# An attention layer's sums begun inside the decay layer before it: grouped decay sums, a norm in two parts, degrees on VectorE

## The chip, the cores and the metric

The kernel runs on one core of one Trainium2 chip. Its time is the device time of one execution in microseconds (us), the median over the runs of one kernel. The engines are called TensorE (matmuls, PE in the profile), ScalarE (ACT), VectorE (DVE), GpSimd (POOL) and SyncE (SP, which issues most of the DMAs). Each works through its own queue and waits on the others by semaphores.

## The reference

A graph network of four layers over N = 3327 nodes with D = 64 features and a 0/1 adjacency matrix of 3327 x 3327, some 0.5% ones. Each layer adds its result to x after `h = relu(layernorm(x))`. Layers 0 and 3 are hyperbolic attention layers; the change leaves their work as it is. Cut to the two middle ones:

```python
# layer 1, decay: a node's last neighbours count, each half as much as the next
support = h @ weight
rank = cumsum(adj != 0, axis=1)
k = minimum(rank[:, -1:], 100)
pos = rank - (rank[:, -1:] - k)
w = (adj != 0) * where(pos > 0, 0.5 ** (k - pos), 0)
x = x + w @ support + bias
# layer 2, attention with two GRU cells (h = relu(layernorm(x)) again)
A = adj - diag(diag(adj))
edge = gru([(A > 0) @ h, (A < 0) @ h], h)
att = softmax(where(A > 0, e_plus, where(A < 0, e_minus, -9e15)))
node = gru((att * A) @ (h @ W), h)
x = x + diag(adj)[:, None] * edge + diag(adj)[:, None] * node
```

Since the adjacency is 0 or 1, the softmax of layer 2 is an average over the neighbours: both cells need only the plain sums `A @ h` and the degrees. The kernel counts whether each entry is 0 or 1 (`ok`, `zo`) and has a general path for other inputs, which doesn't run here.

## The kernel before, in words

The nodes are padded to 26 blocks of 128 (T = 26, NP = 3328). The transposed adjacency is kept on chip as 13 pairs of masks in an 8-bit type (`masks`), which layers 1 to 3 use. Features stand as `X[p, t, d]` (node t * 128 + p), in two halves o = 0, 1 of 13 blocks each.

**Decay, `plain_decay` (L1358).** Work goes in 52 steps: c = 0, 1 is a half of the columns, and inside it the blocks b run from 25 down to 0. Step k needs one adjacency tile of 832 KB (`quarters(k)`, 128 x 2 x 832). Tiles 0 to 11 are made into masks during layer 0; tiles from 12 on are loaded into seven buffers in rotation (`bufs`: four made in layer 0 and three more). `make_mask(k)` turns a tile into its mask, on GpSimd or, for some tiles, on VectorE, three steps ahead; `check(k)` counts its zeros on VectorE and then loads tile k + 7 into the buffer. A list `LATE` names 12 tiles that aren't checked here; they are loaded again in the attention layer and checked there.

A step's TensorE work is counting and summing. `counts(k, o, after)` adds, into a PSUM tile `cnt[o]`, how many neighbours come later than each one; ScalarE's exponential (`weights`, L1425) makes the decay's weights `w` from it; `counts(k, o, rest)` brings the counter forward to the next block, and so must wait until that exponential has read it. `sums(k)` (L1430) multiplies the weights with the features of block b, given as two 16-bit parts, into `acc[c]`. Steps 0 to 11 only count, while the features are being made (L1549 to L1558). From k = 12 the loop at L1540 runs counts of step k and sums of earlier steps: two sums each step ahead of the counts until it has caught up, later one sum between the counts. The weights `w` lie in 13 places: ten inside masks not yet made and three of their own. When a half is done, `degrees` (L1441) reads the degrees from `cnt[o]` on ScalarE, `out_of` copies the sums to `outP`, and `from_pairs` multiplies them with the layer's weights and adds the result to X, in pieces: for the first six blocks of each half inside the loop (k = 29, 32), for the other seven after it.

**Attention, `plain_gat` (L1606).** First the norm of all 26 blocks (`norm_relu`, L136: sums, centred values, squares on ScalarE, a square root with a correction, then h and its two 16-bit parts), then on the first of TensorE's banks the product of two small weight matrices (L1643 to L1649: transpose of `wg`, a ScalarE copy `wgT`, a matmul, a ScalarE copy into `wx`), then the sums: 26 blocks of 16 matmuls (L1708) with b from 25 to 0, and between the blocks, by the table `todo`, transposes of H (`turn`), corrections of the degrees (`degrees`), the late checks and the inverse of the degrees (`inverse`). Then eight steps of the two GRU cells (2 cells x 4 column pieces, L1776 to L1794: `products` on TensorE, `sigmoids`, `tanh` on ScalarE, `before_tanh`, `state` on VectorE), and last `from_pairs`, which turns the result, scales it by the diagonal and adds it to X (L1796 to L1803).

**What sets the order.** Layer 0 opens a region with `tc.manual_schedule` for ScalarE, VectorE, TensorE and GpSimd (L576), in which every engine's queue has the order in which the Python text issues the instructions; `plain_decay` runs in it. `plain_gat` is called after that region has ended and opens its own for ScalarE, VectorE and TensorE (L1632), around the norm, the sums and the GRU steps; its last `from_pairs` stands outside, so that the planner places those instructions. DMAs on SyncE go out in order, each when its buffer is free.

## Time and profile before

| what | value |
| --- | --- |
| median of 3 runs (lowest, highest) | 750.41 us (749.41, 752.73) |
| the profiled execution | 750.64 us |
| its span, first to last instruction | 748.8 us |
| TensorE busy (matmul), VectorE, ScalarE, GpSimd | 634.7, 518.6, 543.1, 467.3 us |
| mean granted TensorE clock | 0.947 |
| layer 0 / decay / attention / layer 3 in the span, about | 0 to 239 / 239 to 393 / 393 to 487 / 487 to 749 us |

"Busy" is the time in which an engine had an instruction under way. The page also gives the chain of work that ended last, followed back from the last instruction; a span on it can be shortened only by shortening what is on it or by starting it earlier. Idle time of an engine off that chain costs nothing. In rows of the timeline, the first number is the start in us and the second the length in us; in the chain too.

### The profile page before, as it was taken

How to read it: one execution, taken by the hardware profiler on the slowest of the kernel's cores; microseconds unless marked ns; L12 is line 12 of the kernel's file. 1: busy time of each engine (PE TensorE's matmuls, PEld its weight loads, DVE VectorE, ACT ScalarE, POOL GpSimd, SP SyncE). 2: the span in 40 equal slices, each digit the busy share in tenths (PEclk: the TensorE clock that was granted, in tenths of full speed). 3: DMA queues.
4: the chain of work that ended last, by engine and by line, in shares of the span. 5: the costliest groups of instructions: out<-in, count | busy, mean ns of one | idle time of the engine just before them, and what ended most of it. 6: DMA issues, size and time to landing. Idle time of an engine off the chain costs nothing.

```text
span 748.8 us, 11837 instructions
## 1 busy us (share of the span) xinstructions
PE 634.7 (85%) x4227; PEld 257.6 (34%) x4227; DVE 518.6 (69%) x909; ACT 543.1 (73%) x697; POOL 467.3 (62%) x353
## 2 busy tenths in 40 slices
PE   0799999999999788889982999328999999999950
PEld 0522233333333333434441663124223333333310
DVE  6867777777777698978828577996555555555556
ACT  2788888888887864577782369257888889889841
POOL 2699989989999002399910000036888788887830
PEclk9999999999999999999995999659999999999995
DMA  3988898988888600599813640001001001000001
GB/s 62 347 261 284 267 279 252 287 273 275 259 261 266 260 1 10 200 401 380 334 36 149 223 143 1 0 0 39 1 1 39 1 2 38 0 1 1 1 2 49
DMA packets 57028, 106.46 MB, mean 142 GB/s; under 512 B 8928, under 2 KB 33152, under 8 KB 56960
## 3 DMA queue, kind: packets, MB, share of 16 engines
q1 hardware_dynamic: 52608, 105.59, 42.5%
q10 hardware_dynamic: 4352, 0.02, 0.3%
q8 instruction: 35, 0.57, 0.3%
q14 instruction: 33, 0.27, 0.1%
HBM read 102.87 MB, written 0.88 MB: 139 GB/s over the span
## 4 chain that ended last, share of the span: by engine, by line
PE 59%; DVE 18%; ACT 8%; issue 7%; POOL 5%; DMA 1%; ACTq 1%; POOLq 0%; DVEq 0%
PE slot L627 16%; PE slot L635 9%; PE slot L608 8%; PE slot L1422 7%; PE slot L609 7%; PE bank L1708 5%; POOL sig L597 5%; PE slot L1436 4%; ACT sig L595 2%; DVE X L1473 2%; DMA adj<-in 1%; DVE mask L1410 1%; ACT slot L614 1%; ACTq L307 1%; ACT w L1428 1%
## 5 line engine op out<-in xcount | busy, mean ns | idle before, releaser
L618 DVE SCALAR_TENSOR_TENSOR sig<-slot,sig 128x768 f32<-128x768 f32 (+1 forms) x208 | 212.7, 1022 | 145.7 <-POOL sig L597 141.7
L614 ACT ACTIVATE slot<-slot 128x768 f32<-128x768 f32 (+1 forms) x208 | 177.3, 852 | 54.4 <-PE slot L609 54.2
L597 POOL TENSOR_TENSOR sig<-adj,sig 128x768 f32<-128x768 f32 (+1 forms) x104 | 201.0, 1962 | 14.2 <-ACT sig L595 10.0
L595 ACT ACTIVATE sig<-leftB,right 128x768 f32<-128x768 f32 (+1 forms) x208 | 203.2, 977 | 0.1
L597 POOL TENSOR_TENSOR sig<-mask,sig 128x768 f32<-128x768 fp8e4 (+1 forms) x104 | 173.2, 1677 | 40.4 <-ACT sig L595 35.0
L627 PE MATMUL slot<-sig,Xr 128*64 128x384 f32 (+1 forms) x832 | 169.6, 526 | 6.3 <-DVE sig L618 6.1
L608 PE MATMUL slot<-XC,XT 128*128 128x384 f16 (+1 forms) x416 | 142.2, 342 | 3.2 <-ACT sum L645 1.7
L609 PE MATMUL slot<-XF,XE 73*128 73x384 f16 (+1 forms) x416 | 141.4, 340 | 0.0
L635 PE MATMUL slot<-sig,X 128*32 128x384 f32 (+1 forms) x832 | 94.2, 525 | 0.0
L1428 ACT ACTIVATE w<-slot,ebias 128x832 bf16<-128x832 f32 x76 | 68.6, 951 | 30.7 <-PE slot L1422 30.6
L627 PEld LDWEIGHTS slot<-sig,Xr 128*64 128x64 f32 x832 | 49.6, 135 | 88.0 <-issue 61.5
L608 PEld LDWEIGHTS <-XT 128*128 128x128 f16 x416 | 40.6, 98 | 93.8 <-issue 67.4
L1422 PE MATMUL slot<-mask,rest 128*128 128x416 fp8e4 x208 | 55.0, 347 | 8.3 <-ACT mask L1428 4.2
L1413 POOL CAST mask<-ahead 128x1664 fp8e4<-128x1664 f32 x17 | 27.8, 1642 | 49.5 <-PE slot L1436 45.1
L1422 PE MATMUL slot<-mask,after 128*128 128x416 fp8e4 x208 | 54.7, 346 | 4.4 <-ACT deg L1443 2.9
L418 POOL MEMSET X<- 128x832 f32 x2 | 1.6, 791 | 84.4 <-ACT xh L1732 84.4
L1333 DVE TENSOR_SCALAR_CACHE_REDUCE same<-ahead 128x832 bf16<-128x832 f32 (+1 forms) x39 | 52.4, 1345 | 0.3
L609 PEld LDWEIGHTS <-XE 73*128 73x128 f16 x416 | 40.8, 98 | 29.7 <-issue 5.6
L1333 DVE TENSOR_SCALAR_CACHE_REDUCE same<-adj 128x1664 bf16<-128x1664 f32 x25 | 47.1, 1882 | 0.6
L1708 PE MATMUL bank<-mask,h 128*64 128x416 fp8e4 x416 | 40.1, 353 | 0.0
L635 PEld LDWEIGHTS slot<-sig,X 128*32 128x32 f32 x832 | 16.4, 108 | 67.7 <-issue 66.1
L1428 ACT ACTIVATE mask<-slot,ebias 128x832 bf16<-128x832 f32 x28 | 26.1, 952 | 11.5 <-PE slot L1422 11.3
(315 smaller groups left out, 636.6 us busy)
## 6 DMA issues: line engine op xcount, KB each, us to landing
adj<-in SPq DMA_DIRECT2D x78, 384.0 KB, 4.5
adj<-in SPq DMA_DIRECT2D x28, 832.0 KB, 6.8
ahead<-in SPq DMA_DIRECT2D x20, 832.0 KB, 8.3
adj<-in SPq DMA_DIRECT2D x27, 512.0 KB, 4.9
ahead<-in SPq DMA_DIRECT2D x32, 416.0 KB, 5.2
leftB<-left SPq DMA_DIRECT2D x6, 384.0 KB, 3.4
XC<-XT SPq DMA_DIRECT2D x12, 96.0 KB, 5.5
X<-in SPq DMA_DIRECT2D x2, 416.0 KB
```

Of the source, the lines that this page charges most:

```text
L595: A.activation(sig, leftB[c], AF.Sigmoid, bias=right[:, b:b + 1])
L597: G.tensor_tensor(sig, adj, sig, op=OP.mult)
L608: PE.matmul(L[:, o, :c[1] * P], XT[:, rows], XC[c][:, o, :], start=True, stop=False)
L609: PE.matmul(L[:, o, :c[1] * P], XE[:KE, rows], XF[c][:, o, :], start=False, stop=True)
L614: A.activation(L, L, AF.Arctan, scale=PA / SX ** 2)
L618: V.scalar_tensor_tensor(sig, slot[:, :, :tiles[k][0][1] * P], PC, sig, op0=OP.add, op1=OP.mult)
L627: PE.matmul(acc[c][o * D:(o + 1) * D, 0, :n], Xr[:, b, :], sigs[k][:, o, :], start=b == 0, stop=b == T - 1)
L635: PE.matmul(acc[c][q:q + 32, 1, :n], X0[:, b - 1 + i, :], w[:, o, :], start=b == 1, stop=b == T - 1, tile_position=(0, q))
L1333: V.tensor_scalar(same, adj, 0.0, 0.0, op0=OP.is_equal, op1=OP.add, accum_out=count)
L1422: PE.matmul(cnt[o][:, h, :BK], w, cols(k, o, h), start=w is after and steps[k][1] == T - 1, stop=True, skip_group_check=True)
L1428: A.activation(ws[k][:, o, :, :], cnt[o][:, :, :BK], AF.Exp, scale=-LN2, bias=ebias)
L1708: PE.matmul(acc[k][o * D:(o + 1) * D, :], w, mask[:, o * HP + k * BK:o * HP + (k + 1) * BK], start=b == T - 1 and i == 0, stop=b == 0 and ...
```

## The change

* **Loop of the decay.** Counts of step k always come first. Sums follow them in groups: in the first half four at every second step (two at the last ones), in the second half four at k = 30, 34, ..., 50 and the last two at k = 52. The weights have five places of their own instead of three.
* **Degrees.** All but the first of the four degree copies move from ScalarE to VectorE.
* **The tiles.** Tiles 39, 43 and 47 leave `LATE`: they are checked in the decay and not loaded again. Two of the seven tile buffers are allocated outside of layer 0's room (`own`); from step 26 on no new tile is loaded into them, and H and its two 16-bit parts are written there.
* **Norm of the first 12 blocks inside the decay.** `normed_h` is a generator whose pieces are issued one per step from k = 33 on, for blocks 0 to 5 of each half; it uses ScalarE's logarithm and exponential for the inverse root. Their table set is loaded at k = 24; the table load for the square root after the loop goes.
* **The attention's sums** take blocks 0, 13, 1, 14, ... in the order in which their norm is ready. `plain_gat` is called from inside the decay's region. Three blocks are issued between the last two `from_pairs` of the decay, then the norm of the other 14 blocks (`finish`), then the small weights' product and blocks 3 to 25 with a new table `todo`. The PSUM banks of the decay are used on. The late tiles are loaded after `finish`.
* **The end of the GRU.** The four pieces of the last `from_pairs` are issued inside the GRU loop after `state(5)`, `state(6)` and `state(7)`, in the ordered region.
* The diagonal products on GpSimd go one per two steps from k = 25 on, instead of one per step.

```diff
-    LATE = *range(EARLY, EARLY + 4), *range(EARLY + 7, 2 * T - 4, 4)
+    BY_V = range(EARLY + 7, 2 * T - 4, 4)
+    LATE = *range(EARLY, EARLY + 4), *BY_V[:5]
...
-            for k in (1, 0, 4, 3, 2):
...
-            own = [pers.tile([P, 2, 2, BK], BF, name=f"w{i}") for i in range(3)]
+            for k, q in ((1, 0), (0, 0), (0, 1), (1, 1), *[(k, q) for k in (4, 3, 2) for q in range(2)]):
+                free.append(masks[k].bitcast(BF)[:, q, :].rearrange("p (o h i) -> p o h i", o=2, h=2))
+            own = [pers.tile([P, 2, 2, BK], BF, name=f"w{i}") for i in range(5)]
...
             def check(k):
                 if k not in LATE:
-                    zeros(same, adj_of(k), zo[:, k:k + 1])
-                load(k + len(bufs))
+                    zeros(same, adjs[k], zo[:, k:k + 1])
+                buf = adjs.pop(k)
+                if k < T or not any(buf is t for t in ah_.own):
+                    load(next(coming), buf)
...
-                A.activation(deg[q, c * CW:(c + 1) * CW].rearrange("p (h i) -> p h i", h=2),
-                             cnt[o][q, :, :BK], AF.Copy, accum_out=zo[q, 2 * T + c:2 * T + c + 1])
+                if c == 0 and o == 0:
+                    A.activation(to, cnt[o][q, :, :BK], AF.Copy, accum_out=total)
+                else:
+                    V.tensor_scalar(to, cnt[o][q, :, :BK], 1.0, 0.0, op0=OP.mult, op1=OP.add, accum_out=total)
...
+            def normed_h(ks, mid, squares):
...
+                V.reduce_sum(s, x, axis=AX.X)
+                yield
+                V.tensor_scalar(s, s, 1.0 / D, None, op0=OP.mult)
+                yield
+                V.tensor_sub(mid, x, wide4(s))
+                yield
+                A.activation(squares, mid, AF.Square)
+                yield
+                V.reduce_sum(v, squares, axis=AX.X)
+                yield
+                V.tensor_scalar(v, v, 1.0 / D, LN_EPS, op0=OP.mult, op1=OP.add)
+                yield
+                A.activation(y, v, AF.Ln)
+                A.activation(y, y, AF.Exp, scale=-0.5)
+                yield
+                V.scalar_tensor_tensor(q, y, -0.5, y, op0=OP.mult, op1=OP.mult)
+                yield
+                V.tensor_mul(q, q, v)
+                yield
+                V.scalar_tensor_tensor(y, q, 1.5, y, op0=OP.add, op1=OP.mult)
+                yield
+                for o in range(2):
+                    V.scalar_tensor_tensor(to[:, o], mid[:, o], 0.0, y[:, o, :, None].to_broadcast([P, n, D]),
+                                           op0=OP.max, op1=OP.mult)
+                    A.activation(hi[:, o], to[:, o], AF.Copy, scale=SH)
+                    yield
+                for o in range(2):
+                    V.scalar_tensor_tensor(lo[:, o], to[:, o], SH, hi[:, o], op0=OP.mult, op1=OP.subtract)
+                    yield
...
-            for k in range(LAG, K_ + 2):
+            norm0 = normed_h(slice(0, T // 4), M[:, :12, :], Xr[:, :12, :])
+            for k in range(LAG, K_ + 1):
                 c, b = steps[min(k, K_ - 1)]
-                if done < k - 1:
-                    for _ in range(2):
-                        sums(done)
-                        done += 1
-                    catching = True
-                else:
-                    catching = False
                 if k < K_:
                     counts_before(k)
-                elif k == K_:
+                else:
                     counts(k - 1, 1, rest)
                     degrees(steps[k - 1][0], 1)
+                if k in (T - 4, T) or k < T and k % 2 == 0 or k > T and (k - T) % 4 == 0 or k == K_:
+                    n = k if k in (T - 4, T, K_) else min(done + 4, k)
+                    for i in range(done, n):
+                        sums(i)
+                    done = n
+                    if done in (T, K_):
+                        out_of(0 if done == T else 1)
...
-                if not catching and done < K_:
-                    sums(done)
-                    done += 1
-                    if steps[done - 1][1] == 0:
-                        out_of(steps[done - 1][0])
...
+                if k == T - 2:
+                    A.preload_act_table_set("natural_log_exp_and_others")
+                if k > T + 6:
+                    next(norm0, None)
+            for _ in norm0:
+                pass
+            drop_diagonal(masks[0][:, 0, :], 0, 0, NP)
+
+            def last_x(i):
                 pt = acc[0][:, i, :].rearrange("p (t h d) -> p t h d", h=2, d=D)
-                from_pairs(None, outP, add, wt, ts, pt)
...
+                from_pairs(None, outP, add, wt, (range(6, 10), range(10, T // 2))[i], pt)
+
+            def finish():
+                for _ in normed_h(slice(T // 4, T // 2), M[:, :14, :], Xr[:, 12:, :]):
+                    pass
...
+            order = [o * C2 + k for ks in (range(T // 4), range(T // 4, C2)) for k in ks for o in range(2)]
...
+            block(0)
+            last_x(0)
+            block(1)
+            last_x(1)
+            block(2)
+            finish()
+            close()
             wk = st.enter_context(room(name="pgl", bufs=4))
...
-                todo = {T - 2: lambda: check(3), T - 4: lambda: turn(0), T - 6: lambda: degrees(0, 1),
-                        T - 7: lambda: check(2), T - 8: lambda: turn(4), T - 10: lambda: degrees(2, 3),
-                        T - 11: inverse, T - 12: lambda: turn(8), T - 15: lambda: turn(12)}
...
+                todo = {4: lambda: turn(0), 5: lambda: check(1), 6: lambda: degrees(0, 1), 8: lambda: check(3),
+                        9: lambda: degrees(2, 3), 11: inverse, 13: lambda: turn(4), 15: lambda: turn(8),
+                        17: lambda: turn(12)}
+                for n in range(3, T):
+                    block(n)
+                    if n in todo:
+                        todo[n]()
...
+                def last(i):
+                    from_pairs(None, oP, use, None, range(4 * i, min(4 * i + 4, C2)),
+                               banks[4 + i].rearrange("p (t h d) -> p t h d", h=2, d=D))
...
-                from_pairs(ps, oP, use)
+                    for i in {C + 2: (0,), C + 3: (1,), C + 4: (2, 3)}.get(u, ()):
+                        last(i)
```

In the diff `V`, `A`, `G` and `PE` are VectorE, ScalarE, GpSimd and TensorE. The small weights' product (`wgT`, `wx`) is unchanged and now stands after `close()` and before block 3.

## The prediction

> **What bounds the kernel now.** I read the page first (span, then the chain by line), then the chain in order of time between 236 and 516 us, where every edited line runs, then the waits there, and last the separate queues of TensorE, ScalarE and VectorE. The two outer layers (0 to 238 and 512 to 749 us) keep their instructions, so only these 275 us are costed. From the chain (start, length, what):
>
> ```profile
> 380.37 1.51 PE slot L1422 x8
> 381.89 0.82 PE slot L1436 x8
> 382.71 1.51 PE slot L1422 x8
> ...
> 387.88 0.95 ACT deg L1443 x2
> ...
> 394.65 1.96 DVE ln_s L144 x2
> ...
> 407.75 0.04 issue
> 407.80 0.90 PE bank L1648 x2
> 408.70 8.02 PE bank L1708 x64
> ...
> 435.27 15.09 PE bank L1708 x170
> 450.38 0.51 ACT xh L1726
> ```
>
> The decay's second half is TensorE work without a hole: 8 counting matmuls and 8 summing ones, 1.51 + 0.82 = 2.33 us a step. Then TensorE leaves the chain for some 19 us (degrees, last outputs, the norm), and the attention's sums run from 408.70 to 450.38. Removing that hole is what there is to win. The waits there say what TensorE resumes on, and the queues show the rhythms that the change runs into (ScalarE, TensorE, VectorE; start, length, operation):
>
> ```profile
> PEld bank L1648 <- ACT wgT L1645: 13.8, 1, 13.8
> ```
>
> ```profile
> 256.16 11.43 ACT L1428 ACTIVATE mask<-slot,ebias 128x832 bf16<-128x832 f32 x12
> ```
>
> ```profile
> 300.79 1.60 PE L1436 MATMUL slot<-mask,h 128*64 128x416 bf16 x16
> 302.32 0.53 PE L1422 MATMUL slot<-mask,after 128*128 128x416 fp8e4 x2
> ```
>
> ```profile
> 324.77 1.89 DVE L1333 TENSOR_SCALAR_CACHE_REDUCE same<-ahead 128x1664 bf16<-128x1664 f32 x1
> ...
> 478.46 0.58 DVE L1773 TENSOR_TENSOR o<-o,gate 128x416 f32<-128x416 f32 x1
> 478.96 0.68 DVE L1801 TENSOR_TENSOR o<-pt,dcol 128x512 f32<-128x512 f32 x1
> 479.56 0.58 DVE L1774 TENSOR_TENSOR H<-o,nn 128x416 f32<-128x416 f32 x1
> ```
>
> TensorE waited for the copy of wgT, which stands in ScalarE's queue behind the norm's copies. In steps without sums (k = 4 to 11) ScalarE sets the pace: 12 exponentials in 11.43 us, so 1.905 us a step. Sixteen summing matmuls take 302.32 - 300.79 = 1.53 us, eight take 0.83: each further eight cost 0.70 and a change of kind 0.13. The last fence is VectorE in step 26 (a check of an adjacency tile) and at the end of the GRU, where the output's L1801 is woven between two operations of one state.
>
> **What the Trainium skill says.** "PSUM — Partial Sum Buffer", Engine vs sequencer instructions: ScalarE's and VectorE's queues are strictly first in, first out, and matmuls start in program order. The 13.8 us agree. "TensorE: Matmul & The Clock Gate", What's actually happening: an idle window of about 3.4 us halves TensorE's clock. Here the granted clock is 0.50 through 408.5 to 413 us, and 64 matmuls take 8.02 us where 64 x 0.088 = 5.6 are due: 2.4 us lost. "ScalarE: Activation LUTs", Table sets: one set holds both ln and exp; the trace's loads are 1.28 us each.
>
> **The change, part by part.** S(k) is the start of step k's first counting pair; before, S27 = 327.92, S30 = 335.60, S34 = 345.62, S50 = 383.06, S51 = 385.40.
>
> *First half, grouped sums.* Up to 298.7 VectorE's norm and masks hold TensorE, unchanged. From there pairs of steps cost 4.42 + 1.91 = 6.3 us with four sums, against 2 x 3.60; but the masks of steps 24 and 25 are ready only at 316.7 and 319.9 (their casts on GpSimd, behind DMA). Sum: 0, S26 near 323.4 (323.57 before). The table load at k = 24 (1.28 us) falls under the sums there, when ScalarE has about 1.4 us free. Without them, +1.3.
>
> *Degrees.* The trace has no 64x832 VectorE copy out of PSUM; L1447's 384 and 512 elements (0.55, 0.69) give about 1.05 plus 0.08 for the accumulator, near ScalarE's 0.86 + 0.20: between -0.1 and +0.3. What matters is the queue: degrees(0,1) stand behind check(26), whose row ends at 326.66, so they end at 327.7 and TensorE's next count starts at 327.8, not 326.29. Sums 24 and 25 and one pair follow: 327.8 + 0.44 + 1.53 + 0.35 = 330.1 for S27, +2.2. TensorE has then waited 3.7 us, so half clock is likely; its cost is 0 to 1.9, I take 1.0 and add it at the end.
>
> *Second half, four sums together.* Three steps without sums cost 3 x 1.905 = 5.72: exp(k) must be read before counts(k, rest), and that before exp(k+1). The step with sums is TensorE's: 0.95 to its last counting pair, 0.44 to the sums, 2.93 for 32 matmuls (0.83 + 3 x 0.70), 0.35 for a pair: 4.67. A cycle is 10.39 against 4 x 2.337 = 9.35: **+1.04**. ScalarE is idle during the sums and cannot run ahead, having two count slots only. So S30 = 330.1 + 3 x 1.905 + 0.3 (six L1268 matmuls, partly in TensorE's slack) = 336.1; S34 = 346.8; S50 = 346.8 + 4 x 10.39 = 388.4.
>
> *norm0 in those steps.* On ScalarE: a square of 768 elements 0.85 (0.68 for 576 in the trace), Ln and Exp 0.45, two 384-element copies 0.92: **+2.2**, all in steps (36, 39, 43, 44) without sums, so nothing hides them. If grouped with sums they would be free. S50 = 390.6, S51 = 395.3: +9.9.
>
> *VectorE's load from k = 33 to 50.* 17 checks of 1.93 (14 before; tiles 39, 43, 47 no longer late), 3 masks (3.8), norm0 (three 768-element passes 2.9, five tiny 1.0, four of 384 at 0.5): 32.8 + 3.8 + 5.9 = 42.5 us, in 50 us of the new steps. It is hidden, but only because steps are longer; against 18 x 2.337 = 42.1 nothing would be left. DMA: five buffers instead of seven from tile 26 on. A tile of 832 KB lands in 6.8 to 8.3 us (the page's medians), then cast 1.57 and check 1.93: at most 11.8 us for five, 2.4 us a tile under the cycle's 2.6: hidden, narrowly. Moved diagonal products stay one per two steps, 0.6 us each, on a GpSimd that ended at 378: hidden.
>
> *The hole.* From S51: last count +2.5, degrees +4.15, sums 50 and 51 until +4.5, outputs to SBUF (2 x 0.47) +5.5, block 0 (16 matmuls, 1.41) +6.0, last_x(0) +7.15, block 1 +8.6, last_x(1) +9.45 and its add +10.1, block 2 +10.9. finish() on 14 tiles (896 elements): sum 1.09, centre 1.09, square 0.96, sum 1.09, six tiny 1.3, Ln and Exp 0.5, two scaled outputs 0.57 each with ScalarE's copies 0.55 behind, and 0.05 to 0.1 per handover: +17.9. Only then ScalarE reaches wgT's copy (0.2), TensorE makes its two wx matmuls (0.9) and goes on with block 3 at +19.0. So three blocks of the twelve are covered, not twelve; TensorE idles 8 us. The rest is the old stretch less three blocks, 41.7 - 4.2 = 37.5, half clock included: the GRU starts at S51 + 56.5 = 451.8, or 452.8 with the 1.0 above; before, 450.38 = S51 + 65.0. The hole gives back 8.5 of 10.9 lost: **+2.4**. The late checks (9 x 1.97, first tile about +20, because its room is the norm's) end near +52: hidden.
>
> *GRU's tail.* Before, from_pairs stood outside the ordered region and was woven in: VectorE's queue at 476 to 484 us has no gap. Now last(0) stands behind state(5) and ahead of products(7) in TensorE's queue. In the old run's times: state(5) ends at 476.23, the transpose of columns 384 to 512 at 476.75 (VectorE idle 0.55), last(0) 477.95; products(7), begun behind it, end at 479.1 (2.4 us, as at 464.5 to 466.9), so before_tanh(7) runs 479.2 to 480.4 (idle 1.3), state(6) to 483.3; last(1) waits 0.8 for its transposes and ends at 485.3, state(7) at 488.2, three transposes at 489.2, last(2) 490.4, last(3) 491.0, against 486.64: **+4.4** (0 if the planner weaves it as before, 5 if more is lost). The sum over zo, 0.22, which was hidden, now stands before layer 3: +0.2. Removed: the Sqrt table load (hidden behind outputs) and two in the inverse (ScalarE had room): 0.
>
> Sum: 2.4 + 4.4 + 0.2 = **+7.0**. The profiled execution took 750.64 (span 748.8 and 1.84 around it), the median is 750.41; 757.6.
>
> **Rivals.** (1) *Faster: the cover holds.* If wgT's copy doesn't stop TensorE, blocks 3 to 11 run under the norm: 8.5 idle and 2.4 of half clock go, 757.6 - 10.9 = 746.7, and if the tail is woven as before, 742.3. It decides where ScalarE's wgT copy runs before +10.9. For it: the block order allows it. Against: the 13.8 us row and the written order. (2) *VectorE is late.* A tile or GpSimd's cast late by a step puts VectorE behind, degrees(1,1) stand behind the last checks, then inverse() and turn(12) (bank 5 waits for turn(4)'s copies, by my times 1 us late already): +5, 762.6. Against: 7 us of slack in the load above. (3) *Small losses don't show.* Tail woven in the gaps and no half clock: 757.6 - 5.4 = 752.2.
>
> **How the numbers follow.** Main 0.60 (own range 754 to 761), rival 1 0.15, rival 2 0.13, rival 3 0.12. The range 746 to 763 leaves out most of rival 1's deep end and rival 2's. A measurement here tells 0.5%, 3.75 us. Faster: 0.15. Same: 0.12 and 0.05 of the main case. Slower: 0.68.
>
> **What would show it.** In the profile after: a cycle of four steps near 10.4 us between 340 and 390; ScalarE's exponentials in 0.95 us rhythm broken by holes at the sums; TensorE waiting some 8 us on wgT between blocks 2 and 3; GRU start near 452; VectorE waits on L1266 and products(7). A cycle below 9.4 us, or block 3 next to block 2, makes the prediction wrong.

## The result and the profile after

The changed kernel is slower: 774.61 us median of four runs (769.59 to 776.46) against 750.35 us, a ratio of 1.031 with a 95% interval of [1.025, 1.036]. The direction was as forecast; the size was not, +24.3 us where the sum gave +7.0. The profiled execution took 776.46 us, the longest of the four, with a span of 774.6 us.

The chain of work of the changed kernel in order of time answers the one shown of before (start in us, length in us, what):

```profile
382.31 1.17 DVE own L1558
...
383.50 0.02 ACT own L1560
...
383.93 0.95 ACT w L1432
...
384.92 2.76 PE slot L1426 x8
387.68 3.38 PE slot L1440 x29
...
411.85 1.10 DVE ln_s L1536
...
419.59 0.12 ACT wgT L1726
...
420.65 5.63 PE slot L1697 x31
...
438.28 0.59 DVE deg L1761
...
449.44 0.66 PE slot L1737 x4
450.10 4.58 PE slot L1697 x16
...
466.00 0.51 ACT xh L1798
```

Before, TensorE alone was on the chain between 360 and 388 us. Now a scaled output of the new norm (`own`, L1558) leads to ScalarE's copy of it (L1560), then to an exponential and only then to TensorE, at half clock (eight counting matmuls in 2.76 us where 1.51 are usual). The GRU starts at 466.0 us, before at 450.4. TensorE's waits from 400 to 470 us, from the waits of the changed kernel (what waited, for whom, total, times, longest):

```profile
PE slot L1729 <- ACT wgT L1726: 6.8, 1, 6.8
PE slot L1748 <- DVE deg L1761: 3.1, 2, 2.4
PE slot L1737 <- ACT xh L1742: 2.1, 1, 2.1
```

The first was forecast. The other two were not: the correction of the degrees and a transpose of H, which waited for nothing before.

ScalarE's rhythm in the second half, from the timeline of the changed kernel (start, length, instruction, and in brackets the idle time before it and what ended it):

```profile
355.65 1.80 ACT L1432 ACTIVATE w<-slot,ebias 128x832 bf16<-128x832 f32 x2 [2.79 <-PE slot L1426]
357.62 1.80 ACT L1432 ACTIVATE w<-slot,ebias 128x832 bf16<-128x832 f32 x2 [0.17 <-PE slot L1426]
359.31 0.83 ACT L1542 ACTIVATE Xr<-M 128x768 f32<-128x768 f32 x1
```

A step without sums takes 357.62 - 355.65 = 1.97 us, 1.905 in the forecast. The square of the norm (L1542) lies among these steps, and the hole of 2.79 us is where TensorE makes four sums together: as forecast.

Stage by stage, in the profiled executions (us from the start of the span; the forecast has its 1.0 us of half clock included):

| stage | before | forecast | after | after less forecast |
| --- | --- | --- | --- | --- |
| start to S51 | 385.40 | 396.3 | 401.83 | +5.5 |
| S51 to block 3 | | 19.0 | 18.8 | -0.2 |
| block 3 to the GRU's start | | 37.5 | 45.4 | +7.9 |
| (S51 to the GRU's start) | 64.98 | 56.5 | 64.2 | |
| GRU's start to X ready | 36.26 | 40.7 | 44.0 | +3.3 |
| X ready to the end of the span | 262.2 | 262.4 | 264.7 | +2.3 |

Of the first 5.5 us, 2.1 are there when layer 0 ends (the first mask of the decay starts at 244.17 instead of 242.04); in other kernels below with the same layer 0 it started between 241.5 and 247.3, so that this is not put down to the change. The last 2.3 us lie behind the last output DMA, and no reason for them was found. That leaves three places to explain: the decay's end, blocks 3 to 25, and the GRU.

### The profile page after: what moved, and what is told of

Same layout as the page of the kernel before. It is cut to its first block, busy times and chain, and to the rows that moved or that the text cites. A ratio compares the mean times of both kernels' runs of the same rounds, so it can differ in the third digit from the quotient of the medians.

```text
span 774.6 us, 11806 instructions
## 1 busy us (share of the span) xinstructions
PE 646.8 (83%) x4227; PEld 267.1 (34%) x4227; DVE 525.8 (68%) x922; ACT 538.0 (69%) x693; POOL 465.4 (60%) x353
## 4 chain that ended last, share of the span: by engine, by line
PE 49%; DVE 17%; ACT 9%; issue 9%; DMA 7%; POOL 6%; SPq 1%; ACTq 1%; POOLq 0%; DVEq 0%
PE slot L628 14%; PE slot L636 8%; PE slot L609 7%; PE slot L610 6%; POOL sig L598 6%; DMA adj<-in 4%; PE slot L1426 4%; PE slot L1697 4%; PE slot L1440 3%; ACT sig L596 2%; ACT w L1432 2%; DMA ahead<-in 2%; DVE X L1481 1%; DVE same L1335 1%; DVE mask L1412 1%
## 5 line engine op out<-in xcount | busy, mean ns | idle before, releaser
L1432 ACT ACTIVATE w<-slot,ebias 128x832 bf16<-128x832 f32 x78 | 70.8, 950 | 37.3 <-PE slot L1426 36.5
L609 PEld LDWEIGHTS <-XT 128*128 128x128 f16 x416 | 40.7, 98 | 93.8 <-issue 67.4
L1426 PE MATMUL slot<-mask,rest 128*128 128x416 fp8e4 x208 | 56.5, 354 | 16.0 <-ACT w L1432 11.1
L1426 PE MATMUL slot<-mask,after 128*128 128x416 fp8e4 x208 | 56.8, 357 | 7.8 <-DVE mask L1412 5.4
L610 PEld LDWEIGHTS <-XE 73*128 73x128 f16 x416 | 40.7, 98 | 29.2 <-issue 5.0
L1335 DVE TENSOR_SCALAR_CACHE_REDUCE same<-adj 128x1664 bf16<-128x1664 f32 x26 | 48.9, 1881 | 2.0 <-DMA adj<-in 1.6
L1697 PE MATMUL slot<-mask,own 128*64 128x416 fp8e4 x416 | 42.8, 366 | 0.0
L1415 POOL CAST mask<-ahead 128x1664 fp8e4<-128x1664 f32 x8 | 13.3, 1669 | 46.6 <-PE slot L1440 43.2
L1426 PEld LDWEIGHTS <-rest 128*128 128x128 bf16 x208 | 19.6, 100 | 47.5 <-issue 39.7
L1415 POOL CAST mask<-adj 128x1664 fp8e4<-128x1664 f32 x13 | 20.4, 1570 | 22.2 <-DMA adj<-in 22.2
```

Of the source, the lines that this page charges most:

```text
L609: PE.matmul(L[:, o, :c[1] * P], XT[:, rows], XC[c][:, o, :], start=True, stop=False)
L610: PE.matmul(L[:, o, :c[1] * P], XE[:KE, rows], XF[c][:, o, :], start=False, stop=True)
L1335: V.tensor_scalar(same, adj, 0.0, 0.0, op0=OP.is_equal, op1=OP.add, accum_out=count)
L1426: PE.matmul(cnt[o][:, h, :BK], w, cols(k, o, h), start=w is after and steps[k][1] == T - 1, stop=True, skip_group_check=True)
L1432: A.activation(ws[k][:, o, :, :], cnt[o][:, :, :BK], AF.Exp, scale=-LN2, bias=ebias)
L1697: PE.matmul(acc[k][o * D:(o + 1) * D, :], w, mask[:, o * HP + k * BK:o * HP + (k + 1) * BK], start=n == 0 and i == 0, stop=n == T - 1 and ...
```

## The experiments

Times are medians; the ratios are to the kernel before, with their 95% intervals. The kernel before was timed again beside each group of runs: its median was 750.35 us beside the changed kernel and 751.5 to 752.2 us later, so that nothing is read from a difference of one or two us between two rows. Each kernel is the changed kernel with the edit that is shown, unless its text says more; a stretch of time is taken from one profiled execution.

| kernel | time, us | ratio |
| --- | --- | --- |
| the changed kernel | 774.61 | 1.031 [1.025, 1.036] |
| one sum per step | 767.83 | 1.022 [1.018, 1.025] |
| small weights' product early | 765.85 | 1.016 [1.012, 1.020] |
| output pieces a GRU step later | 769.28 | 1.023 [1.020, 1.027] |
| corrections ahead of the checks | 776.59 | 1.032 [1.030, 1.035] |
| one sum per step, late copies | 766.57 | 1.018 [1.012, 1.024] |
| first degrees on ScalarE | 771.25 | 1.026 [1.022, 1.030] |
| one sum per step, 12 late tiles | 770.10 | 1.023 [1.018, 1.029] |
| banks of different tiles | 767.25 | 1.019 [1.014, 1.025] |
| one sum, late copies, six buffers | 761.24 | 1.015 [1.011, 1.019] |
| changed kernel with six buffers | 769.88 | 1.023 [1.019, 1.027] |
| all behind block 0 mended | 754.13 | 1.003 [1.001, 1.005] |
| all edits together | 745.35 | 0.991 [0.989, 0.994] |

### One sum per step

```diff
-                if k in (T - 4, T) or k < T and k % 2 == 0 or k > T and (k - T) % 4 == 0 or k == K_:
+                if k in (T - 4, T) or k < T and k % 2 == 0 or k > T:
```

> The changed kernel with one edit: in the decay's second half one sum per step between the counts, as before the change; all else as changed. Theory A (ScalarE paces the steps that have no sums, 10.4 us per four steps against 9.35, and its norm pieces are laid bare there): S30 to S42, 32.4 us in the changed kernel, falls to 28 to 29, and block 0 starts some 6 us earlier than at 406.2. Theory B (VectorE and the landing of tiles set the pace in this stretch, whatever TensorE's order): the same stretch stays within 1 us of 32.4 and the end moves by less than 2. From the whole, A expects 774.6 - 6 = 768.6 us, B 773 or more.

Measured: 767.83 us. Until sum 43 the rhythm is 2.34 us a step again, the 9.35 us per four steps of before. Then TensorE stops. Its timeline in this kernel, then ScalarE's:

```profile
371.15 0.89 PE L1440 MATMUL slot<-w,h 128*64 128x416 bf16 x8
378.75 0.85 PE L1426 MATMUL slot<-mask,rest 128*128 128x416 fp8e4 x2 [6.70 <-ACT w L1432]
```

```profile
377.33 0.52 ACT L1560 ACTIVATE own<-own 128x384 f16<-128x384 f32 x1 [7.31 <-issue]
377.76 1.78 ACT L1432 ACTIVATE w<-slot,ebias 128x832 bf16<-128x832 f32 x2
```

The exponentials that TensorE needs stand behind a copy of the norm, and that copy waits 7.31 us for VectorE, which reaches its input only at 376.70. From sum 42 to sum 51 it takes 29.4 us, where the rhythm gives 20.45. So theory A holds for the price of the grouping, and theory B for the stretch from step 43 on: the four-step grouping had hidden most of a second bound. Undoing it wins 6.8 us in the medians; in the profiled executions the decay, from its first mask to block 0, is 4.4 us shorter (157.6 for 162.0), and layer 0 happened to end 2.7 us earlier.

Why VectorE is late is seen beside GpSimd. VectorE, then GpSimd, same kernel:

```profile
371.09 0.74 DVE L1553 TENSOR_TENSOR ln_q<-ln_q,ln_v 128x12 f32<-128x12 f32 x1
...
373.56 1.42 DVE L1555 SCALAR_TENSOR_TENSOR ln_y<-ln_q,ln_y 128x12 f32<-128x12 f32 x1
```

```profile
370.23 1.57 POOL L1415 CAST mask<-adj 128x1664 fp8e4<-128x1664 f32 x1
...
373.38 1.57 POOL L1415 CAST mask<-adj 128x1664 fp8e4<-128x1664 f32 x1 [1.21 <-DMA adj<-in]
```

Operations on 12 elements a partition take 0.74 and 1.42 us; the same lines on 14 elements take 0.17 us in the norm after the decay, where GpSimd is idle. They end at 371.83 and 374.98, and GpSimd's casts at 371.80 and 374.95. The Trainium skill, "SBUF — State Buffer", section "Who interferes with whom", says that a VectorE instruction with two inputs in SBUF contends with a GpSimd instruction that reads SBUF, and that their shared ports are an exclusive lock; these rows agree. No run takes the casts away, so that it stays a reading of the rows.

### The small weights' product early

```diff
             block(0)
             last_x(0)
+            PE.transpose(bank(6)[:D, :D], wg, ident[:D, :D])
+            A.activation(wgT, bank(6)[:D, :D], AF.Copy)
             block(1)
             last_x(1)
+            pt = bank(7)
+            PE.matmul(pt[:D, :3 * D], wgT, wx[:D, :, :].rearrange("k g m -> k (g m)"), start=True, stop=True)
+            A.activation(wx[:D, :, :].rearrange("k g m -> k (g m)"), pt[:D, :3 * D], AF.Copy)
             block(2)
             finish()
```

> The changed kernel with one edit: the small weights' product (the transpose giving wgT, its copy, the product into wx and its copy) stands between blocks 0 and 2 instead of behind the norm of the last 14 blocks. Theory: TensorE's wait of 6.83 us between blocks 2 and 3 goes, and with it the half clock of blocks 3 and 4 (2.8 us): the GRU starts 7 to 9.6 us earlier than at 466.0, the whole 774.6 - 8 = 766.6 us. Rival (the stretch is bound by VectorE and ScalarE, which are behind the norm, the checks and the inverse): the wait only moves to the diagonal's and the turns' banks, the GRU starts less than 3 us earlier, 772 or more.

Measured: 765.85 us. Blocks 2 and 3 now run without a hole. Block 0 to the end of the last block takes 53.7 us instead of 60.1; these 6.5 us are a little under the theory's 7 to 9.6, because a part of the wait moves to the second of the diagonal's products. (The medians differ by 8.8 us, the profiled executions by 7.0: sums 42 to 45 happened to be 2.6 us quicker in this one, and layer 0 3.1 us longer.) TensorE's timeline:

```profile
423.83 0.56 PE L1749 MATMUL slot<-diag,ones_bf 128*64 128x416 bf16 x2 [4.56 <-DVE deg L1762]
```

The correction that it waits for stands on VectorE behind the norm of 14 blocks and a late check that waited for its DMA. Both the theory and the rival have their share.

### Output pieces a GRU step later

```diff
-                    for i in {C + 2: (0,), C + 3: (1,), C + 4: (2, 3)}.get(u, ()):
+                    for i in {C + 3: (0, 1), C + 4: (2, 3)}.get(u, ()):
```

> The changed kernel with one edit: the first output piece last(0) is issued one GRU step later, after products(7), together with last(1). Theory (products(7) stood behind last(0) in TensorE's queue and VectorE waited 3.0 us for its gate): the stretch from the GRU's start to the last addition to X falls from 44.0 to 40 to 41.5, the whole to 771.5. Rival (what is lost there is VectorE's own work, 4 x 1.28 us of output after the last state): 43 or more, the whole 774.

Measured: 769.28 us; GRU's start to X ready 39.5 us instead of 43.6 (from the last block's end). In the changed kernel, TensorE's products of step 7 and VectorE's wait for their gate read:

```profile
494.48 3.04 PE L1813 MATMUL slot<-xh,gw 128*64 128x416 f32 x8
```

```profile
495.31 0.69 DVE L1853 TENSOR_TENSOR X<-X,x 128x512 f32<-128x512 f32 x1
499.01 0.65 DVE L1831 SCALAR_TENSOR_TENSOR nn<-slot,gb,gate 128x416 f32<-128x416 f32 x1 [3.01 <-ACT gate L1825]
```

With the edit, the same products start at 482.90, take 1.62 us, and VectorE's L1831 follows without a wait. The theory holds.

### Corrections ahead of the checks

```diff
-                todo = {4: lambda: turn(0), 5: lambda: check(1), 6: lambda: degrees(0, 1), 8: lambda: check(3),
-                        9: lambda: degrees(2, 3), 11: inverse, 13: lambda: turn(4), 15: lambda: turn(8),
-                        17: lambda: turn(12)}
+                todo = {4: lambda: turn(0), 5: lambda: degrees(0, 1), 7: lambda: degrees(2, 3), 8: lambda: turn(4),
+                        9: lambda: check(4), 11: inverse, 12: lambda: turn(8), 15: lambda: turn(12)}
```

> The changed kernel with one edit, the table of what stands between the attention's blocks: all four corrections of the degrees ahead of the first four late checks, the turns of columns 4 to 7 and 8 to 11 moved ahead (before and right behind the inverse). Theory (the 7.9 us that blocks 3 to 25 took over the forecast are TensorE's waits on the diagonal's banks behind the checks, 3.1 us, on a turn's copies behind the inverse, 2.1 us, and the half clock that follows, 2.8 us): block 3 to the GRU's start falls from 45.35 to 38 to 40, the whole to 768. Rival (the late checks' DMAs come later and VectorE is busy to the end anyway): at the end VectorE's inverse and last checks hold the GRU's start, 44 or more.

Measured: 776.59 us, and block 3 to the last block's end 46.7 us (45.7 in the changed kernel). Neither text is right (the rival's 44 us or more came, but not by its reason). VectorE doesn't hold the GRU's start, but the order alone doesn't help. TensorE's timeline:

```profile
434.15 0.37 PE L1748 MATMUL slot<-diag,ones_bf 128*64 128x416 bf16 x2 [0.68 <-DVE deg L1761]
...
453.31 0.47 PE L1737 MATMUL slot<-ident,own 128*128 128x128 f32 x1 [6.13 <-ACT xh L1742]
```

ScalarE's, in the same kernel, with the copies out of bank 5 and those out of bank 4:

```profile
437.15 2.40 ACT L1742 ACTIVATE xh<-slot 64x512 f32<-64x512 f32 x4
...
450.86 2.40 ACT L1742 ACTIVATE xh<-slot 64x512 f32<-64x512 f32 x4
```

Even with VectorE free, each second product of the diagonal waits 0.68 us, the length of one correction. And the last turn, which writes bank 5, waits 6.13 us until 453.3, when ScalarE ends its copies of *bank 4*; those of bank 5 had ended at 439.55. The two banks should have been independent. They are the two halves of one PSUM tile of the decay; before, each bank was a tile of its own.

### Banks of different tiles

```diff
-                    pt = bank(4 + t0 // 4 % 2)
+                    pt = bank((4, 7)[t0 // 4 % 2])
...
-                    dg = bank(6 + k % 2)[:, :BK]
+                    dg = bank((6, 5)[k % 2])[:, :BK]
...
-                               banks[4 + i].rearrange("p (t h d) -> p t h d", h=2, d=D))
+                               banks[(4, 6, 5, 7)[i]].rearrange("p (t h d) -> p t h d", h=2, d=D))
```

> The changed kernel with one edit: what alternates between two PSUM banks (the turns, the diagonal's products, the four last output pieces) alternates between banks of two different PSUM tiles (4 and 7, 6 and 5; the last pieces 4, 6, 5, 7) and no longer between the two halves of one tile. Theory (the program waits for the other half's reader because the decay's PSUM tiles hold two banks each and are taken as one): TensorE's waits on the diagonal (0.69 and 2.45 us) and on a turn's copies (2.05 us) go, block 3 to the last block's end falls from 45.7 to 41 to 43, the last pieces lose 0.5 to 1 us, the whole 774.6 - 4.5 = 770. Rival (these waits follow from the queue's order whatever the bank): waits and stretch unchanged within 0.7 us, the whole 774.

Measured: 767.25 us. TensorE's waits from 400 to 470 us in this kernel:

```profile
PE slot L1729 <- ACT wgT L1726: 6.8, 1, 6.8
PE slot L1818 <- DVE deg L1799: 2.0, 1, 2.0
PE slot L1737 <- ACT xh L1742: 0.8, 1, 0.8
```

The waits on the diagonal are gone, though the checks still stand ahead of the corrections; that on a turn is down from 2.1 to 0.8 us. Block 3 to the last block's end takes 39.2 us instead of 45.7, and the GRU 42.3 instead of 43.6. The theory holds, at more than its price. Only the choice of banks was changed, so the waits come from what the program takes for one buffer, not from the order of the queues.

### One sum per step, late copies

The first kernel again, with the scaled outputs issued first, three steps of nothing, then ScalarE's two copies:

```diff
                 for o in range(2):
                     V.scalar_tensor_tensor(to[:, o], mid[:, o], 0.0, y[:, o, :, None].to_broadcast([P, n, D]),
                                            op0=OP.max, op1=OP.mult)
-                    A.activation(hi[:, o], to[:, o], AF.Copy, scale=SH)
                     yield
+                for _ in range(3):
+                    yield
+                for o in range(2):
+                    A.activation(hi[:, o], to[:, o], AF.Copy, scale=SH)
+                    yield
```

> The kernel with one sum per step (of the first experiments), with one more edit: in the norm inside the decay, ScalarE's two copies are issued three steps after VectorE has been given the second scaled output, not in the same step as their input. There TensorE stood still for 6.70 us at 372 to 378.75, and sums 42 to 45 took 18.3 us where 9.35 are due. Theory A (the exponentials stand behind a copy that waits for VectorE): that stretch falls to 9.4 to 10.5 us, and block 0 starts near 390 instead of 399.1, the whole 767.8 - 9 = 759. Theory B (VectorE itself is late: the mask of step 43 ended at 378.2, where TensorE wanted it at 372.7): 14.5 us or more remain there, the whole 764 or more.

Measured: 766.57 us, 1.3 us less than without the edit, inside both intervals. ScalarE's stall is gone (sums 42 to 45 keep their rhythm, to within 0.1 us), but TensorE now waits a few steps on for the masks themselves. Its timeline:

```profile
380.62 0.51 PE L1426 MATMUL slot<-mask,after 128*128 128x416 fp8e4 x2 [1.00 <-DVE mask L1412]
...
384.98 0.51 PE L1426 MATMUL slot<-mask,after 128*128 128x416 fp8e4 x2 [1.86 <-POOL mask L1415]
```

Sum 42 to sum 51 takes 23.8 us, 29.4 before the edit, 20.45 at full pace. Block 0 starts at 396.0, not at 390 (2.2 us of that lie in layer 0, which ended later in this execution). Theory A names the stall of sums 42 to 45 rightly; theory B, wrong for these four (9.4 us where it had 14.5 or more), is right that the masks are late as well, and the whole is where it put it, not at 759.

### One sum per step, 12 late tiles

```diff
-    LATE = *range(EARLY, EARLY + 4), *BY_V[:5]
+    LATE = *range(EARLY, EARLY + 4), *BY_V
```

> The kernel with one sum per step, with one more edit: tiles 39, 43 and 47 are checked late in the attention, as before the change; VectorE has three checks of 1.93 us less in the decay. Theory (VectorE has more work there than steps of 2.34 us allow): sums 42 to 45, 18.3 us, shrink by 2 to 4 us and sums 46 to 51 stay at pace; the whole 767.8 - 3 = 765. Rival (the landing of tiles in five buffers sets VectorE's pace): VectorE's waits on DMA grow by what its work shrinks, the stretch stays within 1 us, the whole 767 to 768. Rival (ScalarE's copies alone): as far as VectorE's own order goes, the same stretch within 2 us.

Measured: 770.10 us, and 31.1 us from sum 42 to sum 51 (29.4 without the edit). Between 328 and 388 us VectorE's busy time falls from 47.3 to 42.3 us, and its waits for tiles grow from 4.7 to 9.6 us (to 392): what it no longer does, it waits for. That is the first rival's mechanism, though its numbers were missed (1 us at most for the stretch, which grew by 1.7): VectorE's pace there is that of the tiles.

### Six buffers

H gets a place of its own, and only one of the seven buffers is given up at step 26 (hP, later, uses the other one):

```diff
-                if k < T or not any(buf is t for t in ah_.own):
+                if k < T or buf is not ah_.own[1]:
...
-            H = ah_.own[0].rearrange("p o i -> p (o i)").rearrange("p (k o d) -> p k o d", o=2, d=D)
+            H = hs_[0]
...
+            hs.append(pool.tile([P, T // 2, 2, D], F32, name='H'))
...
-            hP = pers.tile([P, HP], F32, name="hP")
+            hP = own[0].rearrange("p o i -> p (o i)")
```

> The kernel with one sum per step and the late copies, with one more edit: H has a place of its own, so that six tile buffers instead of five are in rotation from step 26 on (one still goes to the two 16-bit parts). Theory (five buffers slow the tiles: 274 GB/s at 348 to 388 us against 399 before the change, GpSimd and VectorE wait 20 us for DMA there): 310 GB/s or more, those waits fall below 14 us, sums 42 to 49 take 19 to 20 us instead of 22.1, the whole 766.6 - 3 = 763.5. Rival (VectorE's queue is too full whatever the buffers): its waits on DMA fall, but the masks come as late, the stretch stays above 21 us, the whole 766.

> The changed kernel with that one edit: six buffers instead of five, all else as changed (four sums together, copies with their input). Theory (late tiles put VectorE behind, and so the copies and the exponentials): sums 42 to 45, 14.8 us in the changed kernel, fall to 10.5 to 12.5, block 0 comes 3 us earlier than at 406.2, the whole 774.6 - 3 = 771.5. Rival (VectorE's count of work in this stretch): 14 us or more remain, the whole 774.

Measured: 761.24 us (with one sum per step and late copies) and 769.88 us (the changed kernel with this edit alone). The stretch from 348 to 368 us in the kernel before, in the changed kernel, and in the first of these two (window, length, busy us and instructions of TensorE, its weight loads, VectorE, ScalarE, GpSimd; TensorE's clock, DMA share, GB/s):

```profile
348.00:368.00 20.00, 20.00 (x138) 9.12 (x138) 16.26 (x16) 15.16 (x18) 19.37 (x27) 1.00 1.02 399
```

```profile
348.00:368.00 20.00, 17.83 (x127) 9.24 (x127) 16.08 (x20) 13.08 (x16) 13.45 (x19) 1.00 0.80 269
```

```profile
348.00:368.00 20.00, 20.00 (x139) 9.12 (x139) 19.74 (x24) 16.15 (x20) 14.50 (x24) 1.00 0.88 314
```

With seven buffers the DMA engines were busy throughout. With five they have gaps: 269 GB/s is 832 KB (0.852 MB) in 3.2 us, more than a step of 2.34 us and more than a quarter of a cycle, 2.6 us. What the loads wait for is VectorE's checks, which give the buffers free. SyncE's waits between 328 and 392 us, before and in the changed kernel:

```profile
SPq L1399 <- DVE same L1333: 24.8, 13, 4.3
```

```profile
SPq L1400 <- DVE same L1335: 46.3, 14, 7.8
```

Read together, it is a circle: late tiles make late checks, and these make late loads. With six buffers and one sum per step, sum 42 to sum 51 takes 20.45 us, full pace to the end of the decay, though 314 GB/s is still 2.7 us a tile: the rate in one window doesn't say by itself where the limit lies. The changed kernel's groups of 32 summing matmuls, then those with six buffers as the one edit:

```profile
373.17 3.00 PE L1440 MATMUL slot<-w,h 128*64 128x416 bf16 x32
...
387.61 3.45 PE L1440 MATMUL slot<-w,h 128*64 128x416 bf16 x32
```

```profile
374.07 3.00 PE L1440 MATMUL slot<-w,h 128*64 128x416 bf16 x32
...
384.77 3.00 PE L1440 MATMUL slot<-w,h 128*64 128x416 bf16 x32
```

The 14.44 us there (12.0 to 15.0 in the other kernels that keep this stretch as it is in the changed one) fall to 10.70, and the copies still stand with their input: it was the tiles that made VectorE late. The theory holds in both kernels; in the first of them VectorE does 19.7 us of work in the 20 us shown, as full a queue as the rival could ask for, and holds nothing.

### First degrees on ScalarE

```diff
-                if c == 0 and o == 0:
+                if c == 0:
```

> The changed kernel with one edit: both degree copies of the first half are on ScalarE, as before the change. Theory (the copy on VectorE holds TensorE's counter, +2.2 us, and the clock falls behind it, +1.0): the end of sum 25 to the end of sum 29, 12.07 us in the changed kernel, falls by some 1 us, S27 (332.5) falls by 2 to 4 us, the whole to 771.5 (774.6 - 3). Rival (what is gained is lost again at VectorE's later delay, between sums 41 and 45): the whole within 1 us of 774.6.

Measured: 771.25 us, 3.4 less than the changed kernel, though the two intervals overlap. The profiles don't put this down to the copy. From the decay's first mask to sums 24 and 25 it takes 82.6 us instead of 84.7, but TensorE had come 2.8 us earlier to the degrees, ahead of anything that the edit touches: its wait for the first copy, which is on ScalarE in both, ends 79.1 us behind the first mask, and 81.9 in the changed kernel. From there to sum 24 the changed kernel is the quicker one, 2.9 us against 3.5. TensorE's wait for the second copy is 1.84 us with ScalarE's; with VectorE's it was 1.21 us in the changed kernel and 1.2 to 3.6 in the others, mostly longer where TensorE came earlier. Two kernels with VectorE's copy in which TensorE came as early as here (one sum per step, with 9 and with 12 late tiles) reach sum 24 after 83.9 us. So VectorE's copy can hold TensorE, as the first part of the theory says, for 1.3 us when TensorE comes early; in the changed kernel's profiled execution it held it for no longer than ScalarE's would have. The half clock, the second part, isn't changed: from sum 24 to the next group it takes 11.68 us in both (from the end of sum 25 to the end of sum 29 11.7 in both, not the 12.07 of the expectation).

### All behind block 0 mended, and all edits together

The first is the changed kernel with the early product, the banks, the late output pieces, and this table (with three checks instead of two inside `inverse`); the second has all of that and one sum per step, late copies, six buffers and the degrees on ScalarE.

```diff
+                todo = {4: lambda: turn(0), 9: lambda: degrees(0, 1), 10: lambda: degrees(2, 3), 11: lambda: turn(4),
+                        12: inverse, 15: lambda: turn(8), 18: lambda: turn(12)}
```

> The changed kernel with its decay left as it is and everything behind block 0 mended: the small weights' product between blocks 0 and 2, PSUM banks alternating between tiles, the output pieces a GRU step later, and the degrees' corrections behind block 9 with the checks behind the inverse. Theory (these are separate losses): 8.8 + 7.4 + 5.3 us off 774.6, 753; block 0 to the GRU's start takes 41 to 43 us instead of 60.1. Rival (what is won at block 3 is lost at VectorE, which has the norm, the checks and the inverse to do in a shorter time): block 0 to the GRU's start takes 46 or more, the whole 758 or more.

> All edits of these experiments at once: one sum per step, late copies, six buffers, first degrees on ScalarE, the small weights' product early, banks of different tiles, the output pieces a step later, corrections behind block 9. Theory (the stalls named are all there are): block 0 at 391 to 394, the GRU at 433 to 437, its length 38.5 to 39.5, the whole 738 to 742, faster than the kernel before. Rival (VectorE is behind at the end of the decay and again behind the norm): block 0 at 396 or later, 46 us or more to the GRU, the whole 748 or more.

Measured: 754.13 us and 745.35 us. In the first, block 0 to the last block's end takes 42.8 us; 20.5 us are won, where the three single edits had won 8.8, 7.4 and 5.3, in sum 21.5: near enough to separate losses, as the theory has it, though the new table is a fourth edit here that was not run alone. The second is a little faster than the kernel before, 0.991 [0.989, 0.994], or 0.9%. TensorE's timeline in it:

```profile
401.04 4.41 PE L1704 MATMUL slot<-mask,own 128*64 128x416 fp8e4 x48
405.39 0.66 PE L1742 MATMUL slot<-ident,H 128*128 128x128 f32 x4
405.97 7.22 PE L1704 MATMUL slot<-mask,own 128*64 128x416 fp8e4 x80
```

Blocks 2 to 6 run while VectorE still norms the other blocks (until 409.6): the cover that the block order makes possible. Block 0 starts at 394.3, the last block ends at 438.2. It is neither the 738 to 742 of the theory nor the rival's 748: the GRU takes 41.9 us instead of 38.5 to 39.5, and layer 0 ended 2.4 us later in this execution than in that of the changed kernel. VectorE's timeline there:

```profile
439.53 1.89 DVE L1335 TENSOR_SCALAR_CACHE_REDUCE same<-adj 128x1664 bf16<-128x1664 f32 x1 [0.92 <-DMA adj<-in]
441.34 0.08 DVE L1335 DVE_READ_ACCUMULATOR same<-adj 128x1 f32 x1
441.46 0.22 DVE L1927 TENSOR_REDUCE ok<-zo 128x1 f32<-128x66 f32 x1
441.60 0.58 DVE L1803 SCALAR_TENSOR_TENSOR deg<-slot,deg 128x416 f32<-128x416 f32 x1
```

The last late check and the sum over `zo` now stand ahead of the GRU's first scaled sums: these start 3.7 us behind the GRU's start, and 1.1 in the changed kernel. These 2.6 us are about what the GRU takes too long. With TensorE 28 us earlier, VectorE's late checks are next.

## Why the prediction was right in direction and wrong in size

The direction was right. In the span the forecast is 18.8 us short, and 14.8 of these lie in three steps: that VectorE's load and the five buffers are hidden (3.6), that blocks 3 to 25 cost what they cost before (7.9), and the size of the GRU's tail (3.3). Step by step:

* **First half, degrees: right in number, in part by luck.** S27 came at 332.48; less the 2.1 us of layer 0 that is 330.4, and 331.1 was forecast. But VectorE was not behind its check, and waited itself 1.15 us for TensorE: the counting behind the second copy began at 328.12, or 326.0 without layer 0's 2.1, where 327.8 was forecast. The half clock came (16 summing matmuls in 2.98 us), and from there to S27 it took 4.4 us, not 2.3 and the 1.0 of half clock. The two errors, -1.8 and +1.1, largely cancel.
* **Four sums together: held.** The group that starts at 373.17 follows its predecessor by 10.49 us; 10.39 was forecast. Undone, 9.35 came back.
* **The norm on ScalarE (+2.2): the square, Ln and Exp held.** The cycles before are 11.16 and 10.94 us. S42 came at 371.88, 369.8 without layer 0's 2.1; the forecast's own terms give 337.1 + 10.7 + 2 x 10.39 + 1.3 = 369.9. Up to there the sum comes out right to 0.1 us, with the two errors above in it.
* **"It is hidden, narrowly" (VectorE's load and the five buffers): failed, +3.6 us from S42 to S51** (29.95 us; 2 x 10.39 + 4.7 + 0.9 = 26.4 were due). The step took 2.4 us a tile from a landing, a cast and a check in a row. The trace has 269 GB/s, 3.2 us a tile. What it left out is the wait between these three: a check stands in VectorE's queue behind masks of later tiles that wait for their own DMA, and behind norm operations that took 0.7 to 1.4 us instead of 0.2 beside GpSimd's casts. How much each of the two adds was not measured apart; with six buffers one such operation still took 1.08 us, and TensorE waited nowhere in this stretch for more than 0.4 us. The late VectorE then reached TensorE through a neighbour: ScalarE's copies were costed as 0.92 us of work and not as instructions that wait in front of exponentials. Rival 2 had named a late tile, but put its price behind the decay. Six buffers alone remove the stall.
* **The hole: held.** Block 3 came 18.8 us after S51 (19.0), TensorE's wait on wgT was 6.8 us (8), only three blocks were covered. The half clock that followed, 5.63 us for the first 31 matmuls, was in the sum.
* **"The rest is the old stretch less three blocks, 37.5": failed, +7.9 us, the largest error.** The step carried a stretch over from the old trace, whose banks were eight separate tiles, while the diff reuses the decay's four tiles of two banks each. Alternating between halves of one tile no longer hides a reader: waits of 3.1 and 2.1 us, and clock lost behind them. Other banks give back 6.5 of the 7.9. The text came near with "bank 5 waits for turn(4)'s copies", but asked only whether that time was late, not which instructions now share a buffer.
* **GRU's tail (+4.4): right mechanism, 3.3 us too small.** last(0) ahead of products(7) was the mechanism; VectorE then waited 3.01 us and not 1.3, since products(7) ran at half clock (3.04 us, not 1.62). Undoing this order gives 4.1 us back. Another 2.1 us lie at the GRU's start: its second state ends 15.25 us behind that start, 13.10 before. There ScalarE's copies out of one bank wait 0.66 us for VectorE's reading of the other half of the tile, and TensorE's products wait 2.04 (0.91 before). The rows look like the same sharing, but banks 0 to 3 were changed in no run, so that this is argued and not shown.
* **The sum over zo, +0.2: wrong but empty.** It ran at 454.4, hidden. The end of the program took 1.8 to 2.5 us longer behind the last computing instruction than before in every kernel but one, the one that has 12 late tiles as before the change; why stays open.

The sum: +5.5 (of which 2.1 in layer 0), -0.2, +7.9, +3.3, +2.3 is +18.8, which is the span of 774.6 less the forecast's 755.8. Of what the prediction named as signs of being right, the cycle near 10.4 us, the holes at the sums and the wait on wgT came; the GRU's start near 452 did not.

## What to carry to other kernels

When a change reuses a buffer or a bank elsewhere, costs from the old trace hold only if the dependences are the same: list for each tile who writes and who reads, whole tiles and not parts of them. When it takes buffers away, divide the bytes by the new time per turn of a buffer, with the waits inside each engine's queue, and compare with the old GB/s; a DMA share below 1 where it was 1 is a sign to look there, and no proof (with six buffers 0.88 cost nothing). And put work whose input may be late on an engine's queue only well behind the time at which the input is surely there: here, a copy of 0.5 us in front of the exponentials cost up to 7.3.

## What was not expected of the hardware

TensorE's half clock came without one long idle stretch. Ahead of 384.9 us in the changed kernel TensorE was busy for 1.7 of 3.85 us, with one wait of 2.14 (another of 1.34 lies ahead of these); the next eight counting matmuls ran at half speed, and the granted clock was 0.53 at 385 to 387. Ahead of 328.1 it was busy for 1.4 of 3.8 us, with waits of 1.17 and 1.21, and the granted clock was already 0.78 in the mean at 326 to 328 and 0.50 behind that. But ahead of 326.3 in the kernel before it was busy for only 0.91 of 3.8 us (waits of 1.04 and 1.85), and the granted clock stayed 1.00 from 322 to 330. So in these traces waits of one or two us close together could halve the clock, and whether they did can't be read from their lengths.
